# Taking every eighth column in the 32x32 transposes, loading weights as rows to all partitions, and an opening of zero matmuls, in a gated cross-attention kernel

## The chip, the cores and the metric

The kernel runs on one core of one Trainium2 chip. The time is that of one execution on the device in microseconds (us); lower is better. Before the change three runs had a median of 996.86 us (996.46 to 997.03). A core has five engines that run beside each other and meet only at semaphores: PE (TensorE, matrix products; its weight loads are listed as PEld), DVE (VectorE), ACT (ScalarE), POOL (GpSimd) and SP (SyncE, which only issues DMAs here). SBUF is the on-chip memory with 128 partitions; PSUM holds the matmul results in eight banks.

## The reference

All data are float32. `x` is (8, 1024, 1024), the memory `ctx` is (8, 64, 512).

```python
memory_proj = einsum('bme,de->bmd', memory, W_mem)            # W_mem  (1024, 512)
scores  = einsum('bnd,bmd->bnm', x, memory_proj) / sqrt(1024)
attn    = softmax(scores, axis=-1)
context = einsum('bnm,bmd->bnd', attn, memory_proj)
gate    = sigmoid(einsum('bnf,df->bnd', concat([x, context]), W_gate) + b_gate)  # W_gate (1024, 2048)
fused   = x + gate * context
out     = fused * rsqrt(mean(fused**2) + 1e-6) * norm_w
```

## The kernel before

**The main loop.** `x` is cut into 16 tiles of 512 rows (QT). For each tile the product of x with the first half of W_gate (W1) is computed by two levels of Strassen-Winograd: seven outer products (`outer_product`, in the order 1, 6, 7, 5, 4, 2, 3 of `ORDER`), each of seven inner products A, B, C, D, A again, E, F of 128x128 by 128x256 blocks in two accumulating matmuls. The sums of blocks of x that they need are made on DVE (`outer_s`: tiles `s`, `a`) and POOL (`inner_s`: tile `l`); the sums of the results are made from PSUM on DVE (`u`, `gate`) and POOL (`gate<-gate,u`). The five PSUM banks b0 to b4 of the inner products are handed on in the order 2, 3, 0, 4, 1 from one outer product to the next, so B of the next product takes the bank of D, C that of A, D that of E, and E that of F. A product can therefore start only when DVE has read the bank's former result. The part of the gate that comes from the context is not computed from the context: `attn` is multiplied by two small matrices per batch, memory_proj itself (`pc`) and memory_proj times the second half of W_gate plus the bias (added into the banks A, F, E, D). Slots, counted in inner products, fix by hand when each piece of work is put into an engine's queue (`plan`, `at`, `mid`); every engine runs its queue in that order.

**The opening.** Before the tiles, the kernel computes memory_proj transposed (tiles `pm`, then `mpT`), stores it, and multiplies it by the second half of W_gate (W2) in eight rounds `pg`, n = 0 to 7. Round n uses bank n mod 5. Its result is read by DVE (`g<-pg,bias_sb`), put into one of three staging buffers (n mod 3) and stored to DRAM (`mgd<-g`), so round 3's read waits for round 0's store. Beside the rounds DVE makes 24 sums and differences of W1's blocks (`w1_tasks`) and then, after round 5, six 32x32-block transposes of x's first tile, and after round 6 the rest (list `first`). All loads are issued on SP's queue, in the order memory half 0, W_mem chunk 0, memory half 1, W_mem chunks 1 to 3, W2, bias, W1, x tile 0, norm_w, and then the stores.

**How features get onto partitions.** PE contracts over partitions, so x, the memory and the weights need the feature index there. x and the memory are loaded with a quarter of the features on each group of 32 partitions (four DMAs of 32 partitions each) and are then transposed on DVE in 32x32 blocks. Each block takes 32 neighbouring columns, so feature d = 256 i + 32 j + r lands on partition 32 i + r of chunk j. The weights must follow the same order: `rows_by_chunk` loads a chunk as four DMAs, each of 32 rows onto 32 partitions, and `order_wm` reorders the columns of W_mem on DVE (contiguous runs of 32 elements).

The functions touched are `rows_by_chunk`, `load_wm`, `transpose_mem`, `order_wm`, `transpose_x` and the round loop. The transposes are at L186 (memory), L247 (memory_proj) and L303 (x).

Of the kernel before, what the change touches and what calls it, by code (L numbers as in the profile page):

```python
# [8 lines left out]
F32 = mybir.dt.float32  # L9
# [6 lines left out]
P = 128  # L16
# [4 lines left out]
def tile_gated_cross_attention_rmsnorm(  # L21
# [7 lines left out]
    norm_w: bass.AP,  # L29
    out: bass.AP,  # L30
):

# [27 lines left out]
    nc = tc.nc  # L62
    B, N, D = x.shape
# [4 lines left out]
    BM = B * M  # L68
    KD = D // P
    KE = E // P  # L70
    H = 512
    C = 256
# [9 lines left out]
    small = ctx.enter_context(tc.tile_pool(name="small", bufs=1))  # L82
    ps = ctx.enter_context(tc.tile_pool(name="ps", bufs=1, space=PSUM))
# [3 lines left out]
    pin = tc.keep_in_program_order  # L87

    def mm(o, lhsT, rhs, start, stop):
        pin(nc.tensor.matmul(o, lhsT, rhs, start=start, stop=stop, skip_group_check=True))  # L90

    def tt(eng, o, a, b, op):
        pin(eng.tensor_tensor(o, a, b, op))  # L93

    def load(o, i):
        pin(nc.sync.dma_start(o, i))  # L96

    def t4k(pool, shape, tag, name):
        return pool.tile(shape, F32, tag=tag, name=name)

    def rows_by_chunk(w):

        return w.rearrange("(i j r) f -> i r j f", i=4, r=32)

    banks = [f"b{i}" for i in range(5)]

    def bank(n, shape, name):
        return ps.tile(shape, F32, tag=banks[n % 5], name=name)

    memq = [t4k(rot, [P, BM // 64, E // 4], "l2", f"memq{i}") for i in range(2)]
# [1 line left out]
        "(g s c) (i e) -> g i c s e", g=2, c=32, i=4  # L114
    )
    wm = t4k(xqpool, [P, KE, D], "xq", "wm")
    wmr = w_mem_t.rearrange("(i j r) d -> i r j d", i=4, r=32)

    def load_mem(g):
        for i in range(4):  # L120
            load(memq[g][32 * i : 32 * (i + 1), :, :], memr[g, i])

    def load_wm(lo, hi):
        for i in range(4):
            load(wm[32 * i : 32 * (i + 1), lo:hi, :], wmr[i][:, lo:hi, :])

    load_mem(0)
    load_wm(0, 1)
    load_mem(1)
    load_wm(1, KE)  # L130
    w2r = rows_by_chunk(w_gate_t[D:, :])
    w2 = []
    for k in range(KD):
        t = t4k(*((gpool, [P, D], "gate") if k < 7 else (apool, [P, D], "s4")), f"w2_{k}")
        for i in range(4):
            load(t[32 * i : 32 * (i + 1), :], w2r[i][:, k, :])
        w2.append(t)
    bias_sb = t4k(small, [P, D], "junk", "bias_sb")
    load(bias_sb, b_gate.partition_broadcast(P))

    w1r = rows_by_chunk(w_gate_t[:D, :])
    w1 = [const.tile([P, 4, D], F32, name=f"w1_{h}") for h in range(2)]
    for h in range(2):
        for i in range(4):
            load(w1[h][32 * i : 32 * (i + 1), :, :], w1r[i][:, 4 * h : 4 * h + 4, :])
    xq = {}

    def load_xq(q):  # L150
# [31 lines left out]
    memT = [t4k(apool, [P, 2, BM], f"a1{i + 1}", f"memT{i}") for i in range(2)]  # L182

    def transpose_mem(g, i):
        pin(
            nc.vector.transpose(  # L186
                memT[i][:, :, g * (BM // 2) : (g + 1) * (BM // 2)].rearrange(
                    "p j (s c) -> p s j c", c=32
                ),
                memq[g].rearrange("p s (j r) -> p s j r", r=32)[:, :, 2 * i : 2 * i + 2, :],  # L190
            )
        )

    wmp = []

    def order_wm(k):
        t = t4k(apool, [P, KD, P], ("a21", "a22", "s1", "s2")[k], f"wmp{k}")
        pin(
            nc.vector.tensor_copy(
                t.rearrange("p j (i r) -> p j i r", r=32),  # L200
                wm[:, k, :].rearrange("p (i j r) -> p j i r", i=4, r=32),
            )
        )
        wmp.append(t)

    transpose_mem(0, 0)
    order_wm(0)
    transpose_mem(1, 0)
    order_wm(1)
    transpose_mem(0, 1)  # L210
    transpose_mem(1, 1)
    order_wm(2)
    order_wm(3)

    mpT = [
        t4k(rot, [P, 2, BM], tag, f"mpT_{tag}_{i}")
        for tag in ("l2", "u")
        for i in range(2)
    ]

    def mp_rows(j, q):
        return mpT[j // 2][:, j % 2, q * P : (q + 1) * P]


    mpq = [t4k(apool, [P, 4, Q4], f"a{i}{j}", f"mpq{i}{j}") for i in (1, 2) for j in (1, 2)]
    pm = [bank(j, [P, BM], f"pm{j}") for j in range(5)]
    pm += [ps_ctx.tile([P, BM], F32, tag="ctx", name=f"pm{j}") for j in (5, 6)]
    pm += [ps.tile([P, BM], F32, tag="sc", name="pm7")]
# [15 lines left out]
    for g in range(4):  # L244
        for j in range(0, KD, 2):
            pin(
                nc.vector.transpose(  # L247
                    mpq[g].rearrange("p s (j r) -> p s j r", r=32)[:, :, j : j + 2, :],
                    mpT[j // 2][:, :, g * P : (g + 1) * P].rearrange(
                        "p j (s c) -> p s j c", c=32  # L250
                    ),
                )
            )
        for i in range(4):
            load(
                mgd[0, g * P : (g + 1) * P, i * Q4 : (i + 1) * Q4].rearrange(
                    "(s c) e -> c s e", c=32
                ),
                mpq[g][32 * i : 32 * (i + 1), :, :],
            )  # L260
# [26 lines left out]
    A, S, L2, O = {}, {}, {}, {}  # L287
    sTs, attns, attnTs, scs, mps, mgs = {}, {}, {}, {}, {}, {}
    KH = KD // 2
# [4 lines left out]
    def transpose_x(q, t, half):  # L294

        key = q, t // 2, half
        if key not in A:
            A[key] = t4k(
                apool, [P, KH, 2 * P], f"a{t // 2 + 1}{half + 1}", f"a{t // 2 + 1}{half + 1}_{q}"
            )  # L300
        r = t % 2
        pin(
            nc.vector.transpose(  # L303
                A[key][:, :, r * P : (r + 1) * P].rearrange("p j (s c) -> p s j c", c=32),
                xq[q].rearrange("p s (j r) -> p s j r", r=32)[
                    :, 4 * t : 4 * t + 4, half * KH : (half + 1) * KH, :
                ],
            )
        )

    def outer_s(q, n):
        a11, a12, a21, a22 = (A.get((q, r, h)) for r in range(2) for h in range(2))
        if n == 3:
            S[q, 3] = a21
            tt(nc.vector, a21, a11, a21, ALU.subtract)
            return
        s = S[q, n] = t4k(apool, [P, KH, 2 * P], f"s{n}", f"s{n}_{q}")
        if n == 1:
            tt(nc.vector, s, a21, a22, ALU.add)
        elif n == 2:  # L320
            tt(nc.vector, s, S[q, 1], a11, ALU.subtract)
        else:
            tt(nc.vector, s, a12, S[q, 2], ALU.subtract)
# [16 lines left out]
    def inner_s(q, o, part):  # L340
        l11, l12, l21, l22 = quarters(left(q, o))
        if part == 0:
            L2[q, o] = t4k(rot, [P, 4, 2, P], "l2", f"l2_{q}_{o}")
        s1, s2, s3, s4 = (L2[q, o][:, i, :, :] for i in range(4))
        if part == 0:
            tt(nc.gpsimd, s1, l21, l22, ALU.add)
            tt(nc.gpsimd, s2, s1, l11, ALU.subtract)
        else:
            tt(nc.gpsimd, s3, l11, l21, ALU.subtract)
            tt(nc.gpsimd, s4, l12, s2, ALU.subtract)  # L350
# [72 lines left out]
    def load_mg(b):  # L423
# [4 lines left out]

    first = [
        *(lambda t=t: transpose_x(0, t, 0) for t in (0, 1)),  # L430
        *(lambda t=t, h=h: transpose_x(0, t, h) for h in range(2) for t in (2, 3)),
        lambda: outer_s(0, 1),
        lambda: outer_s(0, 2),
        *(lambda t=t: transpose_x(0, t, 1) for t in (0, 1)),
    ]
    done, n = 0, 0
    for h in range(2):
        cols = slice(h * H, (h + 1) * H)
        for q in range(NPAIR):
            pg = bank(n, [P, H], f"pg2_{h}_{q}")  # L440
            for k in range(KD):
                mm(pg, mp_rows(k, q), w2[k][:, cols], k == 0, k == KD - 1)
            stage = t4k(small, [P, H], ("mg", "attnT", "mpb")[n % 3], f"g2_{h}_{q}")
            tt(nc.vector, stage, pg, bias_sb[:, cols], ALU.add)
            load(mgd[1, q * P : (q + 1) * P, cols], stage)
            if n < 5:
                while done < len(w1_tasks) * (n + 1) // 5:
                    w1_tasks[done]()
                    done += 1
            elif n == 5:  # L450
                for f in first[:6]:
                    f()
                for part in range(2):
                    inner_s(0, 1, part)
            elif n == 6:
                for f in first[6:]:
                    f()
            n += 1
    load_mp(0)
# [328 lines left out]
```

## Time and profile before

The profile shows one execution. Its own time was 994.48 us, of which the span from the first to the last instruction is 992.7 us.

| what | value |
|---|---|
| median of 3 runs | 996.86 us |
| profiled execution, own time / span | 994.48 / 992.7 us |
| PE busy | 967.9 us (98%) |
| DVE busy | 770.7 us (78%) |
| POOL busy | 688.4 us (69%) |
| ACT busy | 319.4 us (32%) |
| L303 transposes of x on DVE | 128, mean 691 ns, 85.8 us |
| first product of the memory stage | starts at 8.23 us |
| first product of tile 0 | starts at 93.94 us |
| one tile in the steady state | 55.0 us |

In a group line such as `L303 DVE STREAM_TRANSPOSE a<-xq 128x512 f32<-128x512 f32 x128` one reads the source line, the engine, the operation, the tile written and the tile read with their shapes, and the count. `L93` and `L90` are the lines of the helpers `tt` and `mm`, so the tile names tell the work apart. A timeline line gives the start, the duration, the work, and in brackets how long the engine had been idle and what ended that. Neighbouring instructions of an engine overlap by some tens of ns in these listings, so the distance from start to start is the better price of one: 0.61 us for an L303 transpose, and 0.215 us for a matmul instruction of 256 columns (a float32 product shows as two).

### The profile page before, as it was taken

How to read it: one execution, taken by the hardware profiler on the slowest of the kernel's cores; microseconds unless marked ns; L12 is line 12 of the kernel's file. 1: busy time of each engine (PE TensorE's matmuls, PEld its weight loads, DVE VectorE, ACT ScalarE, POOL GpSimd, SP SyncE). 2: the span in 40 equal slices, each digit the busy share in tenths (PEclk: the TensorE clock that was granted, in tenths of full speed). 3: DMA queues.
4: the chain of work that ended last, by engine and by line, in shares of the span. 5: the costliest groups of instructions: out<-in, count | busy, mean ns of one | idle time of the engine just before them, and what ended most of it. 6: DMA issues, size and time to landing. Idle time of an engine off the chain costs nothing.

```text
span 992.7 us, 14303 instructions
## 1 busy us (share of the span) xinstructions
PE 967.9 (98%) x4944; PEld 765.2 (77%) x4944; DVE 770.7 (78%) x1494; ACT 319.4 (32%) x588; POOL 688.4 (69%) x851
## 2 busy tenths in 40 slices
PE   6998999999999999999999999999999999999995
PEld 4444888888788888888888888888887888888873
DVE  2547777878788787878797887878787887878787
ACT  0000214234242415233333425142342434161444
POOL 0001676868788786868787787868687887868772
PEclk9999999999999999999999999999999999999998
DMA  9994618192835647191926556381927465382612
GB/s 211 234 234 157 128 30 173 64 181 96 143 93 117 146 102 164 54 201 65 171 77 130 123 125 142 80 189 50 181 85 138 117 128 117 89 188 62 172 65 85
DMA packets 72248, 126.76 MB, mean 128 GB/s; under 512 B 13040, under 2 KB 49904, under 8 KB 72176
## 3 DMA queue, kind: packets, MB, share of 16 engines
q1 hardware_dynamic: 63536, 94.39, 37.6%
q0 software_dynamic: 8640, 31.46, 17.0%
q8 instruction: 39, 0.64, 0.3%
q14 instruction: 33, 0.27, 0.1%
HBM read 85.98 MB, written 39.85 MB: 127 GB/s over the span
## 4 chain that ended last, share of the span: by engine, by line
PE 86%; DMA 5%; DVE 4%; SPq 2%; issue 1%; ACT 0%; POOL 0%; DVEq 0%; ACTq 0%
PE kA L90 19%; PE pc L90 12%; PE kE L90 11%; PE kF L90 10%; PE kD L90 10%; PE kC L90 10%; PE kB L90 9%; PE psT L90 6%; DMA w<-in_w_gate_t 3%; SPq L96 2%; DVE gate L93 1%; DMA mgd<-mpq 1%; DVE a L303 0%; DMA mgd<-g 0%; DMA memq<-in_mem 0%
## 5 line engine op out<-in xcount | busy, mean ns | idle before, releaser
L93 POOL TENSOR_TENSOR gate<-gate,u 128x256 f32<-128x256 f32 x336 | 270.1, 833 | 119.9 <-DVE u L93 117.9
L93 POOL TENSOR_TENSOR l<-a 128x256 f32<-128x256 f32 x128 | 125.7, 982 | 154.3 <-DVE a L303 90.6
L524 ACT ACTIVATE gate<-gate 128x512 f32<-128x512 f32 x128 | 79.0, 629 | 397.0 <-DVE gate L93 397.0
L90 PE MATMUL pc<-mg,attnT 64*128 64x256 f32 x512 | 127.4, 389 | 0.0
L553 DVE SCALAR_TENSOR_TENSOR gate<-gate,ss,nw_sb 128x512 f32<-128x512 f32 x120 | 124.7, 1048 | 1.1
L90 PE MATMUL kB<-it,l 128*128 128x256 f32 x448 | 115.1, 379 | 0.0
L90 PE MATMUL kD<-it,l 128*128 128x256 f32 x448 | 115.0, 379 | 0.0
L90 PEld LDWEIGHTS pc<-mg,attnT 64*128 64x128 f32 x512 | 90.7, 186 | 29.7 <-issue 21.2
L90 PE MATMUL kA<-w,a 128*128 128x256 f32 x384 | 98.7, 380 | 0.4 <-ACT u L668 0.4
L90 PEld LDWEIGHTS kB<-it,l 128*128 128x128 f32 x448 | 85.1, 190 | 11.7 <-POOL l L93 0.3
L90 PEld LDWEIGHTS kD<-it,l 128*128 128x128 f32 x448 | 85.2, 190 | 11.5
L93 DVE TENSOR_TENSOR gate<-gate,pc 128x512 f32<-128x512 f32 x128 | 87.0, 680 | 5.9 <-ACT gate L524 5.9
L303 DVE STREAM_TRANSPOSE a<-xq 128x512 f32<-128x512 f32 x128 | 85.8, 691 | 0.0
L90 PEld LDWEIGHTS kA<-w,a 128*128 128x128 f32 x384 | 71.7, 190 | 10.2 <-ACT u L668 0.8
L93 POOL TENSOR_TENSOR l<-s 128x256 f32<-128x256 f32 x96 | 75.4, 785 | 4.4 <-issue 2.5
L93 DVE TENSOR_TENSOR u<-u,kB 128x256 f32<-128x256 f32 x112 | 46.7, 417 | 33.7 <-PE kB L90 28.4
L90 PE MATMUL kE<-it,a 128*128 128x256 f32 x256 | 69.0, 392 | 0.0
L90 PE MATMUL kC<-w,l 128*128 128x256 f32 x256 | 65.8, 379 | 3.1 <-DVE g L93 3.1
L90 PE MATMUL kA<-t,s 128*128 128x256 f32 x256 | 67.4, 386 | 0.0
L90 PE MATMUL kF<-w,l 128*128 128x256 f32 x256 | 65.7, 379 | 0.0
L93 DVE TENSOR_TENSOR gate<-gate,kE 128x256 f32<-128x256 f32 x112 | 45.2, 416 | 25.5 <-PE kE L90 18.6
L668 ACT COPY u<-kA 128x256 f32<-128x256 f32 x112 | 40.5, 362 | 76.1 <-PE kA L90 73.9
(102 smaller groups left out, 1963.2 us busy)
## 6 DMA issues: line engine op xcount, KB each, us to landing
xq<-in_x SPq DMA_DIRECT2D x64, 512.0 KB, 10.0
gate<-in_x POOLq DMA_DIRECT2D x60, 512.0 KB, 8.1
out<-gate SPq DMA_DIRECT2D x60, 512.0 KB, 2.6
w<-in_w_gate_t SPq DMA_DIRECT2D x32, 128.0 KB, 4.3
w<-in_w_gate_t SPq DMA_DIRECT2D x8, 512.0 KB, 14.8
mg<-mgd SPq DMA_DIRECT2D x16, 256.0 KB, 4.0
mgd<-mpq SPq DMA_DIRECT2D x16, 128.0 KB, 2.6
mgd<-g SPq DMA_DIRECT2D x8, 256.0 KB, 2.1
```

Of the source, the lines that this page charges most:

```text
L90: pin(nc.tensor.matmul(o, lhsT, rhs, start=start, stop=stop, skip_group_check=True))
L93: pin(eng.tensor_tensor(o, a, b, op))
L96: pin(nc.sync.dma_start(o, i))
L303: nc.vector.transpose(A[key][:, :, r * P : (r + 1) * P].rearrange("p j (s c) -> p s j c", c=32), xq[q].rearrange("p s (j r) -> p s j r", r ...
L524: pin(nc.scalar.activation(g, g, AF.Sigmoid))
L553: nc.vector.scalar_tensor_tensor(g[:, cols], g[:, cols], rstd[:, t % 2 : t % 2 + 1], nw_sb[:, cols], ALU.mult, ALU.mult,)
L668: pin(nc.scalar.copy(p1, kb["A"]))
```

## The change

Each 32x32 block now takes every eighth column (every fourth for the memory and W_mem's features) instead of 32 neighbours. Feature d = 8 p + j then lands on partition p of chunk j, so a partition's weights are eight neighbouring rows, and a weight chunk is loaded by one DMA to all 128 partitions. On the DVE side the transposes of the memory and of x read with a stride of 4 or 8 elements and write runs without gaps; the transposes of memory_proj read without gaps and write with a stride of 8. The reordering of W_mem's columns moves from DVE (four copies of 1024 elements) to ACT (eight copies of 512 elements, stride 8). W_mem's first two chunks are issued on ACT's queue, the rest on SP's. Before everything else DVE clears a 128x256 tile and PE multiplies it nine times by itself into a bank that is overwritten later. In the round loop, two transposes of x and the first block sums come after round 4 and all others after round 5; before, they came after rounds 5 and 6.

```diff
-    def rows_by_chunk(w):
-        return w.rearrange("(i j r) f -> i r j f", i=4, r=32)
+    def rows_by_chunk(w, n):
+        return w.rearrange("(p j) f -> p j f", j=n)
+    def chunks(t, n):
+        return t.rearrange("p s e -> p (s e)").rearrange("p (m j) -> p j m", j=n)
...
+    zeros = t4k(small, [P, C], "junk", "zeros")
+    pin(nc.vector.memset(zeros, 0.0))
+    pz = ps.tile([P, C], F32, tag="sc", name="pz")
+    for _ in range(9):
+        mm(pz, zeros[:, :P], zeros, True, True)
...
     load_mem(0)
-    load_wm(0, 1)
+    for k in range(2):
+        pin(nc.scalar.dma_start(wm[:, k, :], wmr[:, k, :]))
     load_mem(1)
-    load_wm(1, KE)
+    load(wm[:, 2:, :], wmr[:, 2:, :])
...
-        for i in range(4):
-            load(t[32 * i : 32 * (i + 1), :], w2r[i][:, k, :])
+        load(t, w2r[:, k, :])
...
-        for i in range(4):
-            load(w1[h][32 * i : 32 * (i + 1), :, :], w1r[i][:, 4 * h : 4 * h + 4, :])
+        load(w1[h], rows_by_chunk(w_gate_t[:D, :], KD)[:, 4 * h : 4 * h + 4, :])
...
-                memT[i][:, :, g * (BM // 2) : (g + 1) * (BM // 2)].rearrange(
-                    "p j (s c) -> p s j c", c=32
-                ),
-                memq[g].rearrange("p s (j r) -> p s j r", r=32)[:, :, 2 * i : 2 * i + 2, :],
+                memT[i][:, :, g * (BM // 2) : (g + 1) * (BM // 2)],
+                chunks(memq[g], KE)[:, 2 * i : 2 * i + 2],
...
-            nc.vector.tensor_copy(
-                t.rearrange("p j (i r) -> p j i r", r=32),
-                wm[:, k, :].rearrange("p (i j r) -> p j i r", i=4, r=32),
-            )
+        for j in (0, KD // 2):
+            pin(nc.scalar.copy(t[:, j : j + KD // 2, :],
+                    chunks(wm[:, k : k + 1, :], KD)[:, j : j + KD // 2]))
...
-                    mpq[g].rearrange("p s (j r) -> p s j r", r=32)[:, :, j : j + 2, :],
-                    mpT[j // 2][:, :, g * P : (g + 1) * P].rearrange("p j (s c) -> p s j c", c=32),
+                    chunks(mpq[g], KD)[:, j : j + 2],
+                    mpT[j // 2][:, :, g * P : (g + 1) * P],
...
-                A[key][:, :, r * P : (r + 1) * P].rearrange("p j (s c) -> p s j c", c=32),
-                xq[q].rearrange("p s (j r) -> p s j r", r=32)[
-                    :, 4 * t : 4 * t + 4, half * KH : (half + 1) * KH, :
-                ],
+                A[key][:, :, r * P : (r + 1) * P],
+                chunks(xq[q][:, 4 * t : 4 * t + 4, :], KD)[:, half * KH : (half + 1) * KH],
...
-            elif n == 5:
-                for f in first[:6]:
+            if n == 4:
+                for f in first[:2]:
                     f()
                 for part in range(2):
                     inner_s(0, 1, part)
-            elif n == 6:
-                for f in first[6:]:
+            elif n == 5:
+                for f in first[2:]:
                     f()
```

## The prediction

> **What bounds the kernel now.** I read the busy shares first, then who waited for whom on PE, then the order of time of the opening, the DMA's rate by stretch, and one tile of the steady state on DVE. PE is busy for 967.9 of 992.7 us. The waits of PE name nearly all that is missing:
>
> ```profile
> PE pm L90 <- DVE wmp L199: 9.2, 2, 8.2
> PE kC L90 <- DVE g L93: 3.1, 1, 3.1
> PE kA L90 <- ACT u L668: 1.6, 3, 1.1
> ```
>
> Columns: total us, times, longest. From 120 us on there is only the third wait, in all 1.6 us. What the opening can give is the first line (8.23 before the first product, 0.96 before W_mem's chunk 1) and the second. In order of time:
>
> ```profile
> 5.32 0.71 DVE L186 STREAM_TRANSPOSE memT<-memq 128x512 f32<-128x512 f32 x1 [5.32 <-DMA memq<-in_mem]
> 7.48 0.69 DVE L199 COPY wmp<-wm 128x1024 f32<-128x1024 f32 x1 [1.46 <-DMA wm<-in_w_mem_t]
> ...
> 65.57 0.68 DVE L93 TENSOR_TENSOR t<-t 128x512 f32<-128x512 f32 x1
> 80.81 0.69 DVE L93 TENSOR_TENSOR g<-pg,bias_sb 128x512 f32<-128x512 f32 x1 [14.55 <-DMA mgd<-g]
> ...
> 97.08 1.30 DVE L303 STREAM_TRANSPOSE a<-xq 128x512 f32<-128x512 f32 x2
> 98.30 0.65 DVE L93 TENSOR_TENSOR g<-pg,bias_sb 128x512 f32<-128x512 f32 x1
> ```
>
> DVE stands still for 14.55 us because round 3's staging buffer waits for round 0's store; that store comes last on a full DMA queue. From 80.81 to 98.95 DVE then works without a pause, and kC of tile 0 waits for the last of it (99.10). So the 3.13 us on PE are late DMA, paid through DVE. The DMA's rate, in the stretches 9 to 31 us (weights, 32 partitions each) and 77 to 81 (stores from 128 partitions); the columns are the stretch, busy time and count of PE, PEld, DVE, ACT, POOL, clock, DMA share, GB/s:
>
> ```profile
> 9.00:31.00 22.00, 21.04 (x62) 12.47 (x61) 3.79 (x6) 0.00 (x0) 0.00 (x0) 1.00 1.04 231
> 77.00:81.00 4.00, 4.00 (x10) 1.71 (x9) 0.19 (x1) 1.28 (x1) 0.00 (x0) 1.00 1.02 401
> ```
>
> The DMA engines are fully busy in both, at 231 and at 401 GB/s. A load to all partitions exists too: the last tile's x, 2 MB, of which the window 921 to 926 us carries the bulk:
>
> ```profile
> DMA packets 494, 1.96 MB, mean 392 GB/s; under 512 B 16, under 2 KB 16, under 8 KB 494
> ```
>
> **The change part by part.** The terms are against the profiled execution, 994.48 us with a span of 992.7.
>
> *Cold start.* Nothing before 8.23 runs on PE. The matmuls by stretches of 2 us after that:
>
> ```profile
> 8.23:10.23 2.00, 2.00 (x5) 1.64 (x6) 0.12 (x1) 0.00 (x0) 0.00 (x0) 1.00 1.17 230
> 10.23:12.23 2.00, 2.00 (x7) 1.57 (x6) 0.59 (x1) 0.00 (x0) 0.00 (x0) 1.00 1.06 209
> 12.23:14.23 2.00, 2.00 (x11) 1.77 (x10) 0.00 (x0) 0.00 (x0) 0.00 (x0) 1.00 1.01 217
> ```
>
> The clock column says 1.00, but the count says half speed for about 4 us. The 32 instructions took 9.11 us; at the later 0.215 us they take 6.88 + 0.17 = 7.05. So 2.06 us are lost, and the zeros take this on themselves: -2.06. They are 18 instructions: by the same rates some 9.6 at 0.43 us (4.1 us) and 8.4 at 0.215 (1.8). The other engines begin at 0.25 to 0.75 us, DVE's clearing some 0.3 (POOL clears half as much in 0.2), so they run from about 1.2 to 7.1.
>
> *The first product's start.* It needs memory half 0 transposed and W_mem chunk 0 reordered by ACT. Lower bound: the memory lands at 5.32 as now, W_mem beside it on the other queue, plus 0.7 us: 6.2, but the zeros hold PE to 7.1. Upper bound: the two queues share the engines, and everything in flight (three quarters of the memory, two chunks: 1.75 MB at 220 GB/s from 2 us) must land first: 10.0 + 0.7 = 10.7. I take 7.4, nearer the lower end, since only 1 MB is needed and half of it goes to all partitions; one MB landed by 7.4 before in the slow form. ACT's copy is 0.63 by its 128x512 row (629 ns); its table load (1.28) stands ahead of the copy's wait and hides under the DMA. -0.83, between 1.1 earlier and 2.5 later.
>
> *Chunk 1.* It was issued after memory half 1, copied at 17.55. Now it is second on ACT's queue, its copies are ACT's third and fourth, over by about 10 us when the need is at 14. -0.96. Chunks 2 and 3 are one DMA behind memory half 1; SP holds it until an earlier transfer has landed, so I put it at 9 us and the landing at 14; need 21.
>
> *The wait of kC.* 10.5 MB of weights go to all partitions. At 231 GB/s they cost 45 us, at 392 27: 18 us. Everything behind moves up: round 0's store, issued at 76.39, would come at about 58, before PE has finished round 3 (66.5, less the 3.85 us of the terms above: 62.7). The 14.55 us go, DVE's block of 18.1 us (80.81 to 98.95) is done at 81, and the last read only waits for PE's round 7 (94.1 - 3.85 = 90.3). That is read by 91.1, and kC is due at 91.9. -3.13. What is late next: `mpb` for tile 0's scores, issued behind round 7's store, 0.45 us after its read, 4.1 us to landing at best: 95.6, against scores due at 96.7 (103.68 - 6.98). Cover 1.1 us; the slowest `mpb` row (6.5 us) would cost 1.3. The new order of the first transposes moves DVE work into idle time and costs nothing; it is covered by the 9 us between 81 and 90. x tile 0 and norm_w move up with the queue; the bias load now also waits for the zeros, which end long before its turn (30.95 us now).
>
> *The strided transposes.* 128 of x (L303), 16 of memory_proj, 4 of the memory. No row of this trace reads or writes with a gap between elements. Below: nothing is gained, the element count is the same and the group already runs as fast as contiguous 512-element work (0.61 against 0.60 us from start to start). Above: two cycles per element, the price of a 1024-element operation, 1.14 us (436.22 to 437.36), so 0.53 more each. I take 0.61, since the same instruction at the same count is the nearest row and DVE's 512-element rows agree whatever their pattern. Against it stands a rule of the Trainium skill, in SBUF — State Buffer, section "Door 1: The DMA port swizzle": a line has 16 bytes, full rate needs two hits on a line, and each crossing pays. At 16 and 32 bytes of stride every element is a new line; if that means twice the time, the page makes it the upper end, 68 us more DVE in all, and the sum becomes that of the second rival below.
>
> Sum: -0.83 - 2.06 - 0.96 - 3.13 = -6.98, 987.5 us. The median shown lies 2.38 above the profiled execution: 996.86 - 6.98 = **989.9 us**.
>
> **The rivals.** *Strided transposes at twice the time, slower.* The opening keeps 6.5 us: its DVE work has the slack above, only ACT's or DVE's first strided piece lies on the start (0.5). The place that decides is the end of each tile:
>
> ```profile
> 418.30 0.42 DVE L93 TENSOR_TENSOR gate<-gate,kD 128x256 f32<-128x256 f32 x1 [0.76 <-PE kD L90]
> 419.33 0.42 DVE L93 TENSOR_TENSOR gate<-gate,kE 128x256 f32<-128x256 f32 x1 [0.60 <-PE kE L90]
> 420.19 0.42 DVE L93 TENSOR_TENSOR gate<-gate,kF 128x256 f32<-128x256 f32 x1 [0.44 <-PE kF L90]
> ...
> 421.13 0.70 DVE L303 STREAM_TRANSPOSE a<-xq 128x512 f32<-128x512 f32 x1
> ...
> 424.12 1.72 DVE L93 TENSOR_TENSOR s<-a,a 128x1024 f32<-128x1024 f32 x1
> 425.87 1.63 DVE L93 TENSOR_TENSOR s<-s,a 128x1024 f32<-128x1024 f32 x1
> 427.43 0.41 DVE L93 TENSOR_TENSOR gate<-gate,kA 128x256 f32<-128x256 f32 x1
> 427.76 0.41 DVE L93 TENSOR_TENSOR gate<-gate,kD 128x256 f32<-128x256 f32 x1
> ```
>
> Four transposes before 417 are swallowed by the three waits shown (1.8 us), all but 0 to 0.25. The two after, at 421.13 and 423.18, leave 1.06 to 1.3 us, and DVE has no wait again before 429. The sum from kD, 427.76 to 428.17, ends at 429.2 to 429.5; with 0.15 us to PE, the next tile's kB, which takes that bank and starts at 428.95, comes 0.4 to 0.65 later. Times 15 tiles: 6 to 10 us, so 996.4 to 1000.4. It decides from 0.43 us per tile (even), and is measurably slower from 0.57.
>
> *The same price, absorbed.* The two `s` sums take 3.35 us where undisturbed ones take 1.22 each; POOL reads at that time. If the delay moves them clear, 0.9 us come back, and no wait appears: 990.4 to 993.
>
> *The clock is not released by zeros, or the start is late.* 2.06 or up to 2.5 us less: 992.
>
> *The loads stay slow, or a store or `mpb` takes the place.* If the weights came no faster, round 3 would still wait until 80.8 and kC until 99: the earlier start would be lost too, 996.9. The 392 GB/s row speaks against it.
>
> **How the numbers follow.** Forecast 0.45, transposes at twice the time and felt 0.28, absorbed 0.15, clock or start 0.06, loads or a new wait 0.06. 0.2%, 2.0 us, is about what a measurement of this kernel can tell from no change. The forecast, the absorbed case and the late start are faster (0.44 + 0.14 + 0.05), with 0.02 from the felt case; that case gives 0.10 same and 0.16 slower; a new wait 0.02 and 0.04; the rest is same. Faster 0.65, same 0.15, slower 0.20. The forecast's own range is 987.9 to 991.7; the range goes to the felt case's upper part, 987.5 to 1000.
>
> **What would show it.** PE: 18 instructions on `zeros` from about 1.2 us, the first product near 7.4 with all its instructions 0.215 us apart, no wait for `g` at kC, kC near 91.9. DMA: some 390 GB/s until W1 is in; no DMA wait on DVE in round 3. L303 at 0.69 us is the forecast; 1.22 the rival, and then the row of PE's waits must show kB on `gate`. Wrong would be the forecast if a wait of PE appears in every tile, or if kC still starts past 95.

## The result and the profile after

The changed kernel takes 992.11 us (median of 6 runs, 990.38 to 993.38), the kernel before 995.43 in the same comparison (6 runs, 992.92 to 997.03): a ratio of 0.9969, 95% interval 0.995 to 0.9989. The profiled execution after took 992.30 us with a span of 990.5, against 994.48 and 992.7. The forecast was 989.9 within 987.5 to 1000.0. So the direction and the range held, but the gain is less than half of the one forecast. Of the four places named for it two gave about what was forecast; the other two, the first product's start and the cold clock, did not. The page, the busy shares:

```profile
PE 972.9 (98%) x4962; PEld 768.9 (78%) x4962; DVE 812.2 (82%) x1491; ACT 327.9 (33%) x596; POOL 688.7 (70%) x851
```

DVE works 41.5 us more than before (770.7), and the time still fell. Who waited for whom on PE (total us, times, longest):

```profile
PE pm L91 <- DVE memT L192: 4.3, 1, 4.3
PE kA L91 <- ACT u L664: 1.6, 3, 1.1
PE pz L91 <- DVE zeros L117: 1.2, 1, 1.2
```

The wait of kC for `g` is gone, as is the second wait of `pm`, for chunk 1. No wait of the steady state has come in their place. But `pm` now waits 4.3 us for the transposed memory, after the zeros are through. PE in order of time (start, duration, work, idle time before and its releaser):

```profile
1.20 5.93 PE L91 MATMUL pz<-zeros 128*128 128x256 f32 x18 [1.20 <-DVE zeros L117]
11.43 29.43 PE L91 MATMUL pm<-memT,wmp 128*128 128x256 f32 x80 [4.30 <-DVE memT L192]
40.70 3.60 PE L91 MATMUL pg<-w,mpT_l 128*128 128x512 f32 x8
...
97.36 1.03 PE L91 MATMUL kC<-w,l 128*128 128x256 f32 x4
```

The zeros run from 1.20 to 7.13, as forecast. The first product starts at 11.43, not 7.4, and 3.20 us later than before (8.23). DVE shows what it waited for, and that the other wait forecast to go did go:

```profile
10.18 1.10 DVE L192 STREAM_TRANSPOSE memT<-memq 128x512 f32<-128x512 f32 x1 [9.04 <-DMA memq<-in_mem]
12.33 3.05 DVE L192 STREAM_TRANSPOSE memT<-memq 128x512 f32<-128x512 f32 x3 [1.05 <-DMA memq<-in_mem]
...
68.36 0.69 DVE L94 TENSOR_TENSOR g<-pg,bias_sb 128x512 f32<-128x512 f32 x1 [2.85 <-PE pg L91]
...
91.35 0.65 DVE L94 TENSOR_TENSOR g<-pg,bias_sb 128x512 f32<-128x512 f32 x1
95.83 0.69 DVE L94 TENSOR_TENSOR g<-pg,bias_sb 128x512 f32<-128x512 f32 x1 [3.83 <-PE pg L91]
```

The first half of the memory is there at 10.18 us; before it was there at 5.32. Round 3's result (68.36) is now read when PE has it, where DVE had stood for 14.55 us for a store. The last read (95.83) waits only for PE. The engines by stretch (busy time and count of PE, PEld, DVE, ACT, POOL; granted clock, DMA share, GB/s):

```profile
8.00:10.00 2.00, 0.00 (x0) 0.00 (x0) 0.00 (x0) 1.28 (x3) 0.00 (x0) 1.00 1.24 203
10.00:12.00 2.00, 0.57 (x2) 0.52 (x3) 1.10 (x1) 1.07 (x2) 0.00 (x0) 0.91 1.14 275
12.00:14.00 2.00, 2.00 (x6) 1.53 (x6) 1.67 (x2) 0.00 (x0) 0.00 (x0) 0.50 1.00 412
14.00:30.00 16.00, 16.00 (x51) 9.68 (x50) 1.39 (x2) 4.19 (x4) 0.00 (x0) 0.97 1.04 422
```

After 4.30 us without work PE's granted clock fell to 0.50, and 6 matmul instructions fall into 2 us where 11 do at full clock (from 16 to 18 us). So the clock that the zeros had released was lost again. The last row shows the loads to all partitions: 422 GB/s, where the weights' stretch before, 9 to 31 us, moved 231.

The difference of the two traces, by marks that both have:

| stretch | before | after | difference |
|---|---|---|---|
| first product starts | 8.23 | 11.43 | +3.20 |
| first product to first `pg` | 30.78 | 29.27 | -1.51 |
| first `pg` to kA of tile 0 | 54.93 | 54.93 | 0 |
| kA to kC of tile 0 | 5.16 | 1.73 | -3.43 |
| kC to the first `psT` | 4.58 | 4.41 | -0.17 |
| first `psT` to the last kF | 877.29 | 877.32 | +0.03 |
| last kF to the end | 11.7 | 11.4 | -0.3 |

They sum to -2.2 us, the difference of the spans. Of the -1.51 us, 0.96 is the wait for chunk 1. So the cold start is only 0.55 us cheaper.

The transposes do cost more. Their group:

```profile
L301 DVE STREAM_TRANSPOSE a<-xq 128x512 f32<-128x512 f32 x128 | 137.8, 1099 | 0.0
```

1099 ns in place of 691, or 1.02 us from start to start in place of 0.61. That is 0.41 each and 52 us on DVE in all, but the table's row of the steady state has not moved.

### The profile page after: what moved, and what is told of

It is laid out like the page before. It is cut to its first block, busy times and chain, and to the rows that moved or that the text cites. A ratio compares the mean times of both kernels' runs of the same rounds, so it can differ in the third digit from the quotient of the medians.

```text
span 990.5 us, 14285 instructions
## 1 busy us (share of the span) xinstructions
PE 972.9 (98%) x4962; PEld 768.9 (78%) x4962; DVE 812.2 (82%) x1491; ACT 327.9 (33%) x596; POOL 688.7 (70%) x851
## 4 chain that ended last, share of the span: by engine, by line
PE 95%; DVE 2%; DMA 1%; issue 0%; ACT 0%; POOL 0%; SPq 0%; DVEq 0%; ACTq 0%
PE kA L91 19%; PE pc L91 12%; PE kE L91 11%; PE kF L91 10%; PE kD L91 10%; PE kC L91 10%; PE kB L91 10%; PE psT L91 6%; PE pg L91 6%; PE pm L91 3%; DVE gate L94 1%; DMA memq<-in_mem 1%; DVE gate L598 0%; PE pa L395 0%; PE sc L369 0%
## 5 line engine op out<-in xcount | busy, mean ns | idle before, releaser
L94 POOL TENSOR_TENSOR l<-a 128x256 f32<-128x256 f32 x128 | 129.1, 1009 | 153.7 <-PE pg L91 89.4
L301 DVE STREAM_TRANSPOSE a<-xq 128x512 f32<-128x512 f32 x128 | 137.8, 1099 | 0.0
L534 ACT ACTIVATE junk<-gate 128x1024 f32<-128x1024 f32 x60 | 63.5, 1058 | 1.5 <-DMA gate<-in_x 0.4
## 6 DMA issues: line engine op xcount, KB each, us to landing
xq<-in_x SPq DMA_DIRECT2D x64, 512.0 KB, 10.1
```

What stands on the lines that cost most here:

```text
L301: nc.vector.transpose(A[key][:, :, r * P : (r + 1) * P], chunks(xq[q][:, 4 * t : 4 * t + 4, :], KD)[:, half * KH : (half + 1) * KH],)
L534: nc.scalar.activation(junk, O[q, t], AF.Square, accum_out=ss[:, t % 2 : t % 2 + 1])
```

## The experiments

The ratios are against the kernel before on the same chip. Its medians there lay at 996.75 to 997.34, somewhat above the 995.43 of the first comparison, and its single runs at 991.5 to 999.3. So the difference of two kernels' medians carries 1 to 2 us that are not the kernels', and where kernels are compared with the changed one, the traces decide.

**1. W_mem on SP's queue.** Why does the memory land 5 us later? Its eight loads are still the first on SP's queue. The theory was that W_mem's transfers on ACT's queue take the DMA engines away from them.

```diff
     load_mem(0)
-    for k in range(2):
-        pin(nc.scalar.dma_start(wm[:, k, :], wmr[:, k, :]))
+    load(wm[:, 0, :], wmr[:, 0, :])
     load_mem(1)
+    load(wm[:, 1, :], wmr[:, 1, :])
     load(wm[:, 2:, :], wmr[:, 2:, :])
```

> The changed kernel with W_mem's chunks back on SP's queue behind the memory's first half (each still one load to all partitions). Theory A (W_mem's two loads on ACT's queue run beside the memory's on the same DMA engines and make it land at 10.1 instead of 5.3 us): the memory's half lands at 5.3 to 5.8, the first product starts at 8.0 to 8.8 instead of 11.43, the zeros' clock is kept, and the time is 4 to 5 us under the changed kernel's, a ratio to before of 0.992 to 0.993. Theory B (the start is late because of ACT's table load or the strided pieces): the first product still starts past 10.5, ratio 0.996 to 0.998.

Measured: 987.86 us (987.69 to 988.03), ratio 0.9917 (0.9895 to 0.9938), span 986.1. DVE's and then ACT's and PE's first work, in order of time:

```profile
5.40 1.09 DVE L192 STREAM_TRANSPOSE memT<-memq 128x512 f32<-128x512 f32 x1 [4.26 <-DMA memq<-in_mem]
```

```profile
7.45 2.12 ACT L204 COPY wmp<-wm 128x512 f32<-128x512 f32 x2 [5.43 <-DMA wm<-in_w_mem_t]
```

```profile
1.19 6.25 PE L91 MATMUL pz<-zeros 128*128 128x256 f32 x18 [1.19 <-DVE zeros L117]
8.61 27.77 PE L91 MATMUL pm<-memT,wmp 128*128 128x256 f32 x80 [1.17 <-ACT wmp L204]
```

The memory is there at 5.40 again, 0.08 us off the time before. PE's first product starts at 8.61, when W_mem's chunk 0 is in and copied, only 1.17 us after the last zeros. The 80 instructions take 27.77 us, against 29.43 in the changed kernel: the clock was kept. So 2.82 us of the start and 1.66 of the clock come back, 4.48 in all, and the medians are 4.25 apart. With this one part undone the kernel beats both, and comes within 0.4 us of the span that the forecast's sum gives (992.7 - 6.98 = 985.7).

Which mechanism of the DMA it is, the records of the changed kernel's first 10 us show (queue, kind, pieces, MB, share of 16 engines; q1 is SP's queue, q10 ACT's):

```profile
q1 hardware_dynamic: 1826, 0.89, 48.9%
q10 hardware_dynamic: 288, 1.05, 36.7%
```

SP's queue moves its bytes in pieces of some 490 bytes, ACT's in pieces of 3.6 KB, on the same 16 engines. From 2 to 4 us the changed kernel's engines carried 188 pieces of the small kind beside 106 of ACT's large ones (0.43 MB); in this experiment's kernel the same two microseconds carried 928 pieces of the small kind, and before 906. The memory's first half is 1024 such pieces (512 KB). So it got a fifth of its former rate while W_mem was under way, and W_mem most of the bytes.

**2. One chunk on ACT's queue.** If that is right, half of the W_mem traffic on ACT's queue must give a delay in between.

```diff
-    for k in range(2):
-        pin(nc.scalar.dma_start(wm[:, k, :], wmr[:, k, :]))
+    pin(nc.scalar.dma_start(wm[:, 0, :], wmr[:, 0, :]))
     load_mem(1)
+    load(wm[:, 1, :], wmr[:, 1, :])
```

> The changed kernel with only W_mem's chunk 0 on ACT's queue; chunk 1 goes to SP's queue behind the memory's second half. Half of the bytes that run beside the memory's first half are taken away. Theory A (the memory's 512-byte pieces wait behind W_mem's 4-KB pieces on shared DMA engines): the memory's first half lands at 7.2 to 8.2, between 5.4 (none beside it) and 10.2 (both), the first product starts at 8.4 to 9.5, and the time lies 2 to 4 us under the changed kernel. Theory B (the queue itself, not the bytes, delays the memory): landing still at 10.

Measured: 988.36 us (988.11 to 988.46), ratio 0.9922 (0.99 to 0.9943). DVE:

```profile
7.98 1.08 DVE L192 STREAM_TRANSPOSE memT<-memq 128x512 f32<-128x512 f32 x1 [6.84 <-DMA memq<-in_mem]
```

5.40, 7.98, 10.18 us with none, one and two chunks on ACT's queue: each costs the memory 2.2 to 2.6 us. W_mem is no longer what the start waits for, but the first product is at 9.21, later than with both on SP's queue, since the memory now comes last. PE was idle for only 0.83 us, and its 80 instructions took 27.75. From 2 to 4 us the engines carried 171 of the memory's pieces here, as few as with two chunks (188): the memory is no faster while W_mem runs beside it, but W_mem is through sooner. That it is the size of the pieces, and not only the bytes of the other queue, that holds the memory back is argued; no run changes the size alone.

**3. Without the zeros.** Were the zeros worth anything where they stood?

```diff
-    zeros = t4k(small, [P, C], "junk", "zeros")
-    pin(nc.vector.memset(zeros, 0.0))
-    pz = ps.tile([P, C], F32, tag="sc", name="pz")
-    for _ in range(9):
-        mm(pz, zeros[:, :P], zeros, True, True)
```

> The changed kernel without the nine products of zeros. Theory A (PE stands idle for 4.3 us after the zeros, so the granted clock falls to half before the real products have run, and the zeros buy nearly nothing): the first product still starts at 11.4, the first 32 instructions take 9.0 to 9.5 us instead of 8.8, and the time is that of the changed kernel, 0 to 0.6 us more: ratio 0.997. Theory B (the zeros do save the half-speed stretch): 1.5 to 2 us slower than the changed kernel, ratio 0.9985 to 0.999.

Measured: 992.89 us (991.92 to 993.53), ratio 0.9967 (0.9953 to 0.9981). PE:

```profile
11.57 30.39 PE L91 MATMUL pm<-memT,wmp 128*128 128x256 f32 x80 [11.57 <-DVE memT L187]
```

The 80 instructions take 30.39 us in place of 29.43. But the ratio is no worse than the changed kernel's 0.9969, and in the profiled executions of experiments 7, 8 and 9, which have the nine zeros at the same place, the 80 instructions take 30.73, 30.44 and 30.66 us. So in the changed kernel the zeros are worth between nothing and 1 us, not 2.06.

**4. Nineteen in place of nine.** If the gap after the zeros loses the clock, zeros that last until the memory is there must keep it.

```diff
-    for _ in range(9):
+    for _ in range(19):
```

> The changed kernel with 19 products of zeros instead of 9, so that PE is busy until about 11.4 us. Theory A: no idle time ahead of the first product, no fall of the clock, the first 32 instructions take 7.0 us, and 1.5 to 2 us less than the changed kernel: ratio 0.995. Theory B (zeros do not hold the clock): no change, 0.997.

Measured: 990.67 us (990.57 to 991.23), ratio 0.9946 (0.9927 to 0.9965). PE:

```profile
1.19 9.94 PE L91 MATMUL pz<-zeros 128*128 128x256 f32 x38 [1.19 <-DVE zeros L117]
11.44 27.75 PE L91 MATMUL pm<-memT,wmp 128*128 128x256 f32 x80 [0.31 <-ACT wmp L204]
```

The start is the same (11.44), the 80 instructions take 27.75 us, 1.68 less than in the changed kernel and 2.64 less than without zeros, and the median lies 2.2 us under that of experiment 3, from the same chip. So the gap was the cause. The runs agree within 0.7 us where those of the changed kernel spread over 3.0, and that goes with the clock too: of the changed kernel's six runs the fastest (990.38) has a mean granted clock of 0.997, the four around 992 have 0.995 or 0.996, and the slowest (993.38) has 0.994; all eight here have 0.996 or 0.997. How long the clock stays halved differs from run to run.

**5. The zeros where they end in time.** The first experiment's kernel, without the zeros:

```diff
-    zeros = t4k(small, [P, C], "junk", "zeros")
-    pin(nc.vector.memset(zeros, 0.0))
-    pz = ps.tile([P, C], F32, tag="sc", name="pz")
-    for _ in range(9):
-        mm(pz, zeros[:, :P], zeros, True, True)
```

> The run with W_mem on SP's queue, without the products of zeros. There PE was idle for only 1.17 us between the zeros and the first product. Theory A (zeros that end shortly before the first product are worth the half-speed stretch, 2.06 us by the profile of before): first product at 8.6 as with them, 32 instructions in 9.0 us or more, 1.8 to 2.3 us slower than with them: ratio 0.9935 to 0.9945, between that run and the changed kernel. Theory B (the clock stays full anyway): no difference, 0.992.

Measured: 990.0 us (989.28 to 991.97), ratio 0.9933 (0.992 to 0.9947). PE:

```profile
8.58 29.40 PE L91 MATMUL pm<-memT,wmp 128*128 128x256 f32 x80 [8.58 <-ACT wmp L199]
```

The start is that of the first experiment (8.58 against 8.61), the 80 instructions take 1.63 us more, and the ratios differ by 0.16%, 1.6 us (the medians, from two chips, by 2.14). So the zeros are worth 1.6 to 2.2 us where the first product follows on them, and at most 1 where it comes 3 to 4 us later.

**6. The loads to all partitions alone.** The kernel before, with only the loads of W1 and W2 changed. The weights then no longer stand on the partitions of their features, so the products are of other numbers, in the same time.

```diff
     def rows_by_chunk(w):
-        return w.rearrange("(i j r) f -> i r j f", i=4, r=32)
+        return w.rearrange("(p j) f -> p j f", j=KD)
...
-        for i in range(4):
-            load(t[32 * i : 32 * (i + 1), :], w2r[i][:, k, :])
+        load(t, w2r[:, k, :])
...
-        for i in range(4):
-            load(w1[h][32 * i : 32 * (i + 1), :, :], w1r[i][:, 4 * h : 4 * h + 4, :])
+        load(w1[h], w1r[:, 4 * h : 4 * h + 4, :])
```

> The kernel before with one part of the change alone: the eight loads of W2 and the two of W1 go to all 128 partitions, one DMA each. The transposes, the opening and the order stay, so the weights' rows are not in the order of x's features; that matching is left out of the computation, the instructions keep their number and shape. Theory A (kC's wait of 3.13 us is late DMA, paid through DVE): the first product starts at 8.2 as before, DVE's wait of 14.6 us in round 3 and kC's wait both go, and the time is 3.1 us under before, ratio 0.9965 to 0.9975, the same as the whole change. Theory B (the loads are hidden, the gain comes from the earlier order of DVE's work): ratio above 0.999.

Measured: 991.03 us (990.86 to 992.05), ratio 0.9951 (0.9931 to 0.9971). All of PE's waits, and then round 3's read on DVE:

```profile
PE pm L90 <- DVE wmp L197: 9.2, 2, 7.9
PE kA L90 <- ACT u L666: 1.6, 3, 1.1
```

```profile
67.58 0.69 DVE L93 TENSOR_TENSOR g<-pg,bias_sb 128x512 f32<-128x512 f32 x1 [2.86 <-PE pg L90]
```

The wait of kC for `g` is gone with the loads alone, and kC starts at 96.58 in place of 99.10. From the first `pg` to kC it takes 56.66 us, exactly as long as in the changed kernel, in place of 60.09. So the whole 3.43 us come from this part. In this execution 0.9 of them are lost again in the memory stage, where the cold clock lasted longer: its first 32 instructions took 9.97 us in place of 9.11. The span is 2.4 us shorter. By the ratios this part alone gains as much as the whole change (0.49% with an interval of 0.29 to 0.69, against 0.31% with 0.11 to 0.50).

The gain by the runs, 4.9 us, is larger than the 2.4 of the two traces, and the granted clocks of the runs point at why. Of the 13 runs of the kernel before beside this experiment, nine have a mean granted clock of 0.993 to 0.995 and took 995.6 to 998.3 us; the other four have 0.996 or 0.997 and took 992.4 to 996.0, and the profiled execution (994.48, 0.996) is of that kind. All six runs of this experiment have 0.996 or 0.997. So in most runs the kernel before loses some clock that is kept when the wait of kC is gone. That the 3.13 us without work at kC lose it is the likely reading; no trace holds an execution in which it happened.

**7. The transposes with neighbouring columns.** The changed kernel, but its transposes of x read 128 neighbouring columns per chunk. x's features are then permuted against the weights.

```diff
-                chunks(xq[q][:, 4 * t : 4 * t + 4, :], KD)[:, half * KH : (half + 1) * KH],
+                xq[q][:, 4 * t : 4 * t + 4, :].rearrange("p s e -> p (s e)").rearrange(
+                    "p (j m) -> p j m", j=KD
+                )[:, half * KH : (half + 1) * KH],
```

> The changed kernel with the 128 transposes of x reading columns that lie side by side; the features of x then stand on other partitions than those of the weights, so the permutation of x is left out of the computation, while all instructions keep their number and shape. Theory A (the slower transposes are absorbed by DVE's idle time): L301 falls from 1.10 to 0.69 us, 52 us of DVE go, and the time stays that of the changed kernel within 1 us, ratio 0.996 to 0.998. Theory B (they are felt): 3 us or more faster, ratio under 0.994.

Measured: 992.28 us (990.56 to 993.63), ratio 0.9962 (0.9947 to 0.9977). The group of the transposes, and three stretches of the opening:

```profile
L301 DVE STREAM_TRANSPOSE a<-xq 128x512 f32<-128x512 f32 x128 | 86.0, 692 | 0.0
```

```profile
10.00:12.00 2.00, 0.63 (x2) 0.57 (x3) 1.10 (x1) 0.97 (x1) 0.00 (x0) 0.65 1.16 269
12.00:14.00 2.00, 2.00 (x6) 1.61 (x5) 1.53 (x2) 0.00 (x0) 0.00 (x0) 0.50 0.97 403
14.00:16.00 2.00, 2.00 (x6) 1.58 (x5) 1.51 (x2) 1.19 (x2) 0.00 (x0) 0.50 1.03 412
```

52 us of DVE's work are taken away again, and nothing is gained: the first `psT` to the last kF takes 877.33 us, against 877.32. The strided transposes are slower, and absorbed. The stretches show the other matter once more. In this execution PE was idle for 3.08 us before the first product, and the halved clock lasted until about 17 us; in the changed kernel's it lasted until about 15.

**8. One transposition more in each tile.** How much of the tile is left? One of the eight strided transposes of a tile is done twice, at one of the two places after 419 us where the prediction put the decision.

```diff
+        for _ in range(2 if half and t == 1 else 1):
...
```

> The changed kernel with one of each tile's eight transposes (the last one, in slot 45) done twice, which puts 1.02 us more in front of the block sums that end DVE's tile. In the changed kernel the sum that frees the bank of the next tile's kB ends 0.58 us before kB starts; 0.15 of that is the way from DVE to PE. Theory A (DVE's slack at that place is 0.43 us per tile): PE waits for kB in each of 15 tiles, 0.3 to 0.6 us each, 4 to 9 us more than the changed kernel, ratio 1.001 to 1.006. Theory B (DVE has slack everywhere): no wait, 0.997.

Measured: 1002.22 us (1001.88 to 1003.14), ratio 1.0058 (1.0038 to 1.0078). A tile takes 55.66 us in place of 55.05; 15 times 0.61 is 9.2 us, and the medians are 10.1 apart. DVE and PE at the end of a tile:

```profile
425.93 2.25 DVE L302 STREAM_TRANSPOSE a<-xq 128x512 f32<-128x512 f32 x2
428.09 0.39 DVE L94 TENSOR_TENSOR u<-u,kD 128x256 f32<-128x256 f32 x1
...
431.54 0.41 DVE L94 TENSOR_TENSOR gate<-gate,kD 128x256 f32<-128x256 f32 x1
```

```profile
428.54 0.70 PE L91 MATMUL kD<-mg,attnT 64*128 64x256 f32 x2
429.16 1.13 PE L91 MATMUL kE<-it,s 128*128 128x256 f32 x4
...
431.99 1.13 PE L91 MATMUL kB<-it,l 128*128 128x256 f32 x4
432.96 1.03 PE L91 MATMUL kC<-w,l 128*128 128x256 f32 x4
```

Against the changed kernel's same stretch, 0.37 us are lost before kE (2.29 us after the context group's start at 426.87, in place of 1.92) and 0.24 between kE and kC (3.80 in place of 3.56). The second is the place that the prediction named: kB starts 0.04 us after DVE's read of kD has ended (431.95). The first and larger is another: the small context product into bank D needs `u<-u,kD` to have read it, and that read stands behind the transposes. The two transposes take 2.16 us from start to start where the one took 1.03, so of 1.13 us added 0.61 reach PE. The slack that was left is some 0.5 us per tile.

**9. Four distances.** At what distance does a transposition become slower? Each tile's eight are made with 1, 2, 4 and 8 elements between the columns, for the row blocks t = 0, 1, 2, 3; x's features are again permuted against the weights.

```diff
+        n = (1, 2, 4, 8)[t]
+        src = xq[q][:, 4 * t : 4 * t + 4, :].rearrange("p s e -> p (s e)").rearrange(
+            "p (c m j) -> p j c m", m=P, j=n
+        )
...
```

> The changed kernel with a different column stride in each of the four transposes of a row of blocks: t = 0 reads every column, t = 1 every second, t = 2 every fourth, t = 3 every eighth (4, 8, 16 and 32 bytes apart). The features of x then stand on other partitions than those of the weights for t = 0 to 2; that matching is left out of the computation. If the price comes with every element that opens a new 16-byte line (a line holds four elements), strides 1 and 2 take 0.69 us, strides 4 and 8 take 1.10. If it grows with the distance, 0.69, 0.8, 0.9 to 1.0, 1.10. If any gap costs the same, 0.69, 1.10, 1.10, 1.10.

One execution, 993.35 us. The first tile's transposes on DVE: first t = 0 and 1, then four with t = 2 and 3, then t = 0 and 1:

```profile
80.05 1.29 DVE L309 STREAM_TRANSPOSE a<-xq 128x512 f32<-128x512 f32 x2
...
83.79 4.04 DVE L309 STREAM_TRANSPOSE a<-xq 128x512 f32<-128x512 f32 x4
...
90.41 1.30 DVE L309 STREAM_TRANSPOSE a<-xq 128x512 f32<-128x512 f32 x2
```

Two of distance 1 and 2 take 1.29 us, as two of distance 1 did before (1.30), and four of distance 4 and 8 take 4.04, as four of distance 8 do in the changed kernel (4.06). Over the kernel the durations lie between 0.667 and 1.109 us. So it is a step between 2 and 4 elements, 8 and 16 bytes, and not a price that grows with the distance.

The Trainium skill, in SBUF — State Buffer, section "Door 1: The DMA port swizzle", has lines of 16 bytes and asks for two hits on a line. The step lies where that rule has it: at 8 bytes two elements share a line, at 16 and 32 none do. The same passage says that one can stride 4 fp32 for free; if that means a distance of 4 elements, these runs do not agree, since there the price is already full. The page has no price for the missing hit; the runs put it at 0.41 us on 0.61, not at twice the time.

**10. More of the same.** The first experiment's kernel with the memory's first half over both queues, W_mem's chunk 0 copied in quarters and ten zeros, to start earlier still.

```diff
-    load_mem(0)
+    for i in range(4):
+        pin((nc.sync if i < 2 else nc.scalar).dma_start(memq[0][32 * i : 32 * (i + 1), :, :], memr[0, i]))
...
-        for j in (0, KD // 2):
+        w_ = KD // 4 if k == 0 else KD // 2
+        for j in range(0, KD, w_):
```

> The run with W_mem on SP's queue, and three more edits: half of the memory's first four DMAs are issued on ACT's queue, W_mem's chunk 0 is copied by ACT in four pieces of 256 elements instead of two of 512, and there are 10 products of zeros. The pieces let the first product start after 0.6 instead of 1.1 us of copying, and the split saves up to 0.9 us of issue time if issue and not the transfer holds the memory back. Expected: first product at 7.6 to 8.2 instead of 8.61, and 0.4 to 1.0 us less than that run, a ratio of 0.991 to 0.9915. If the transfer holds it back: 8.1 to 8.2 and 0.4 us.

Measured: 989.52 us (987.21 to 991.25), ratio 0.993 (0.9906 to 0.9953). PE:

```profile
8.33 3.72 PE L91 MATMUL pm<-memT,wmp 128*128 128x256 f32 x16
12.23 24.32 PE L91 MATMUL pm<-memT,wmp 128*128 128x256 f32 x64 [0.18 <-DVE memT L193]
36.38 3.60 PE L91 MATMUL pg<-w,mpT_l 128*128 128x512 f32 x8
```

A miss: the median lies 1.7 us above the first experiment's (the ratios are 0.993 and 0.9917), not below it. The start is 0.28 us earlier (8.33), and the memory's first half, now in pieces of one size on both queues, is there at 4.99 us in place of 5.40. But the memory's second half is transposed from 11.07 us in place of 10.28, PE waits for it at 12.23, and the first `pg` starts at 36.38 against 36.22 in the first experiment. The profiled spans are 986.2 and 986.1; why its other runs spread over 4 us has no trace to show it.

## Why the prediction was right, and where not

- **The wait of kC: right.** Forecast -3.13 us; kA to kC fell by 3.43, DVE's 14.55 us are gone, and experiment 6 shows that the loads to all partitions do it by themselves. The DMA moved 422 GB/s in the weights' stretch, where the last tile's x had given 392 for the estimate. `mpb` did not take the place: no wait for it is in the list.
- **Chunk 1: right.** -0.96; the wait is gone.
- **The first product's start: wrong, and outside its own bounds.** The term was -0.83 (7.4 us), with an upper bound of 10.7. It was +3.20 (11.43). The step that failed is the lower bound's premise, "the memory lands at 5.32 as now, W_mem beside it on the other queue", and the choice near it "since only 1 MB is needed". The two queues do not share by need: the memory's 512-byte pieces fell behind W_mem's 4 KB pieces. The upper bound had the right mechanism, everything in flight lands first, and its landing at 10.0 was within 0.2 us of the 10.18 measured. What it left out is the price after the landing: 0.7 us were taken for the transposition, which took 1.10, and PE started 1.25 after DVE did.
- **The cold start: wrong by its dependence on the term before.** The -2.06 supposed that the zeros end just ahead of the first product. They did end at 7.13, within 0.1 us of the forecast, and then PE stood for 4.30 us and the clock fell back. What is left of the term is 0.55 us in this trace, and by experiment 3 it can be nothing. With zeros that last until the first product the term is there: 1.6 us (experiments 1 and 5) to 2.2 (experiments 3 and 4). The two terms were added as if independent, and the rival "the clock is not released by zeros, or the start is late" was priced at one of the two losses, up to 2.5 us; together they cost 4.03 + 1.51 = 5.5 against the forecast's sum.
- **The strided transposes: price wrong, effect right by another reason.** They were taken at 0.61 us, "since the same instruction at the same count is the nearest row". They cost 1.02. The upper end, 1.14, was nearer. (The sum of that end is the one of the first rival in the prediction's list, not of the second, as it says.) The case that came is the rival "the same price, absorbed" at 0.41 in place of 0.53, and only in part for the reason that it gave. The changed kernel's end of a tile on DVE:

```profile
418.29 0.42 DVE L94 TENSOR_TENSOR gate<-gate,kF 128x256 f32<-128x256 f32 x1 [0.44 <-PE kF L91]
...
421.47 1.10 DVE L301 STREAM_TRANSPOSE a<-xq 128x512 f32<-128x512 f32 x1
422.50 0.38 DVE L94 TENSOR_TENSOR u<-u,kD 128x256 f32<-128x256 f32 x1
422.80 1.34 DVE L94 TENSOR_TENSOR s<-a,a 128x1024 f32<-128x1024 f32 x1
424.17 1.63 DVE L94 TENSOR_TENSOR s<-s,a 128x1024 f32<-128x1024 f32 x1
...
426.06 0.41 DVE L94 TENSOR_TENSOR gate<-gate,kD 128x256 f32<-128x256 f32 x1
```

  The first `s` takes 1.34 us in place of 1.72. The read of kD ends at 426.47, and the next tile's kB starts at 427.05, so 0.58 us lie between them, where 0.78 did before (428.17 to 428.95). So the shorter `s` gave 0.38 us of the six transposes' 2.5, the slack before kB 0.20, and DVE's waits before the tile's end swallowed most of the rest: of the 1.80 us of the three waits that the prediction shows, 0.44 are left. Experiment 7 shows that the 52 us cost nothing, experiment 8 that one more transposition per tile would have been felt. Experiment 8 also shows a place that the prediction did not name: the context product into bank D, which waits for `u<-u,kD` behind the transposes. That the shorter `s` is due to less reading by POOL at that time was argued in the prediction and is not shown by a run.
- **The sum.** -6.98 forecast for the profiled execution, -2.18 measured. The 4.8 between them are 4.03 (start) and 1.51 (clock), less 0.30 at kC and 0.44 in the small rows of the table. That the median came within 2.2 us of the forecast all the same is luck. The forecast added 2.38 us because the median before lay that far above the profiled execution; after the change it lies 0.19 below it. That distance was no constant of the kernel: the runs of experiment 6 point at a clock that most runs of the kernel before lose and the profiled one kept. And the likeliest case rested on transposes that cost no more, while they cost 1.02 and were absorbed.

## What to carry to other kernels

A load that the first product needs should not share the DMA engines with a bulk load on another queue: with both in order on one queue the first one landed at 5.40 us, with two chunks beside it at 10.18. (The bulk load here came in pieces of 3.6 KB and the other in pieces of 490 bytes; other sizes were not tried.) Matmuls on zeros pay only when the real work follows on them, so their number goes by the landing of the data, and the two terms are to be priced as one. Before calling a dearer instruction harmless or harmful, look for how much wait each stretch of the loop can swallow: 0.41 us on each of eight transposes of a tile were free here, and one more transposition in each cost 9 to 10 us in all.

## What the hardware showed that was not expected

- **The clock falls back soon, and not by the gap's length alone.** Idle gaps of 0.31, 0.83 and 1.17 us after the zeros, and one of 1.30 us in experiment 6, left the granted clock at 1.00; gaps of 3.08, 3.11, 3.40 and 4.30 us after the zeros were followed by 0.50, until 4 to 6 us after the first product's start. But the 3.13 us for which PE stood before kC (95.97 to 99.10 us) in the profiled execution of the kernel before left it at 1.00, as that kernel's stretch from 97 to 112 us shows. No run has a gap between 1.30 and 3.08. The Trainium skill, in TensorE: Matmul & The Clock Gate, section "Part 1: The HAM clock gate (the "warmup" mystery)", puts the loss at one idle window of about 3.4 us; here 3.08 was enough after the zeros, and 3.13 was not at kC.

```profile
97.00:112.00 15.00, 12.88 (x75) 10.51 (x76) 11.04 (x21) 1.12 (x3) 6.73 (x8) 1.00 0.87 176
```

- **The granted clock's column is no record of the first cold microseconds.** It says 1.00 from the first matmul on in every kernel here, while the zeros' instructions run at half rate until 4 to 7 us, as the count per stretch shows. After a gap it does show 0.50.
- **Distance between elements on DVE and ACT.** On DVE 8 bytes cost nothing, 16 and 32 bytes the same +0.41 us for 512 elements per partition. On ACT only 32 bytes were tried: its eight strided copies of 128x512 took 1.114 us on the mean, where its plain 128x512 row takes 0.629.
- **Two queues, one set of engines.** With 1 MB on ACT's queue the memory's loads took 5.6 to 7.9 us from issue to landing, where they had taken 2.5 to 4.0, though the first of them were issued at the same 0.75 us.
